# A two-layer transformer on one core: the rotation sums of the first attention issued behind the scores, and its output products cut into halves spread over the steps

## The chip, the cores and the metric

The kernel runs on one core of one Trainium2 chip. The metric is the device time of one execution in microseconds; three runs of the kernel before the change gave 754.88 to 755.31, median 755.07. All traces are of one profiled execution. The granted TensorE clock is full in every slice of it.

Engines are named as in the profile: PE is the matrix engine (PEld its weight loads), DVE the vector engine, ACT the scalar engine, POOL GpSimd, SP the engine that issues the DMAs.

## The reference, cut to what matters

Input x is 4 sequences of 256 tokens, 256 wide. Two layers follow one another, each an attention and a feed-forward block, each on the normed x and added to x. The change touches the first attention alone:

```python
q = einsum('btd,ndh->btnh', x, q_kernel)            # 16 query heads of 128
k, v = einsum('bsd,ckdh->cbskh', x, kv_kernel)      # 8 key/value heads of 128
q = apply_rope(rms_norm(q, q_norm_scale), positions)
k = apply_rope(rms_norm(k, k_norm_scale), positions)
# apply_rope: x1, x2 = halves of the head;  [x1*cos - x2*sin, x2*cos + x1*sin]
logits = einsum('btkgh,bskh->bkgts', qg * ATTN_SCALE, k)   # causal, window of 128
enc = einsum('bkgts,bskh->btkgh', softmax(logits), v)
out = einsum('btnh,nhd->btd', enc, out_kernel)             # 2048 -> 256, added to x
```

The remaining blocks (a gated feed-forward block with a 2-of-4 choice, a second causal attention, a gated block with a Walsh-Hadamard transform) come after it and are the same in both kernels.

## The kernel before, in words

Everything is f32. Each f32 matmul shows as two MATMUL entries in the trace, called passes here.

The first attention is `attention0`. Its work is cut into 16 units n = 4b + g: b is the sequence, g a group of four query heads with their two key/value heads. `pipelined` runs 20 steps. In step s, stage k works on unit s minus its lag, in a given order of stages, and then what `behind` holds for that step is issued. The order in which the code issues is a priority. The framework's scheduler makes of it one fixed order for each engine, and sets the semaphores; where `tc.issue_after(ins)` stands, an instruction is put behind `ins` on its engine.

The stages before the change, with lags:

- `project` (0), which calls `project0`: for both halves t of the tokens (128 each) two products `pj` (L426; four query heads, then keys and values). DVE multiplies them by the tables into `qs` and `qc` (L431), ACT squares them (L436) and copies `v` (L438). Then for both t: the rotation sum `qc += qs` with the halves of the head swapped (L443) and the sum of the squares `ss` (L444). For units from the seventh on (n >= 6) POOL splits the rotated queries into 16-bit planes `qpl` (L242, a helper's line) and SP transposes them by DMA to `qplT`. POOL then makes the norm factors `ve` (L457, L460) and `r` (L463, a power) and scales the keys, called K below (L466).
- `turn` (1), which calls `turn0`: queries by PE transposes `tr_q` (L481) and DVE copies (L482) for n < 6, by DVE copies out of `qplT` (L486) later; keys by PE transposes `tr_k` (L492) and ACT copies `kT` (L493).
- `score` (2): `probabilities` makes the scores `sc` (L204, L205). DVE adds the mask and takes the maximum in one pass, `mx` (L207). Then come `nb` (L214), exponentials on ACT (L217), the reciprocal `rs` (L222), and the scaling of `p` on POOL (L225).
- `split` (3): `p` into planes `pl` on POOL (L242), transposed by DMA to `plT`. `join` (4): copies to `pT` on ACT (L262); the last three units use PE transposes `tr_p` (L237) instead. `attend` (4): products `av` with the values (L380, L384), copied to `zT` by ACT (L388).

`out(b, t)` is the output product for one sequence and one half of its tokens: 16 matmuls (L294) over the four `zT` of the sequence, and one DVE addition to x (L299). `behind` puts these in steps 8, 9, 12 and 13 for the first two sequences; the four of the last two sequences stand at the end, in step 19, two of them as filler from the last projection on (`kept`).

PSUM has two pools of four banks each here: `half` (the `pj`, the `tr_q`, and `tr_k` for 6 <= n < 14) and `bank` (`sc`, `av`, `po`, `tr_n`, `tr_p`, and the other `tr_k`). The tiles `qc` have 4 buffers, `qs` and `sq` 2 each, `v` 5, `pl` and `plT` 4 together.

The order of the stages in a step is the last argument of `pipelined`: project, attend's `join`, `split`, `score`, `turn`, `attend`.

Of the kernel before, what the change touches and what calls it, by code (L numbers as in the profile page):

```python
# [27 lines left out]
P = 128  # L28
# [20 lines left out]
def two_layers(ctx, tc, consts, tables, x, wq, wkv, wo, w_gate, w_up, w_down,  # L49
# [26 lines left out]
    def bank(shape, name):  # L76
        return ps1.tile([P, *shape], F32, tag="bank", name=name)
# [238 lines left out]
    def attention0():  # L316
        with tc.tile_pool(name="attn0", bufs=2, reuse_waits="tile", side="right") as own:
            xnT, factors = {0: normed(0)}, {}


            cos_s = own.tile([P, NT, 2, HD], F32, name="cos_s", bufs=1)
            sin_s = own.tile([P, NT, 2, HD], F32, name="sin_s", bufs=1)
            with tc.issue_after(last_of["norm"].ins):
                for t in range(NT):
                    for tab, at in ((cos_s, 0), (sin_s, 256)):
                        src = angles[:, at + t * HD : at + (t + 1) * HD]
                        nc.vector.tensor_tensor(
                            tab[:, t], src.unsqueeze(1).to_broadcast([P, 2, HD]), scl, ALU.mult
                        )

            def project(n, _):
                b, g = divmod(n, 4)
                held = project0(own, xnT[b], g, cos_s, sin_s, n >= 6)
                if g == 1 and b + 1 < B:
                    factors[b + 1] = moments(b + 1)
                if g == 2 and b + 1 < B:
                    with tc.issue_after(last_of["qc"].ins):
                        xnT[b + 1] = normed(b + 1, factors[b + 1])
                return held

            def turn(n, held):
                rot, qT_planes, v, r = held
                return *turn0(own, rot, qT_planes, half if 6 <= n < 14 else bank), v, r

            def score(n, held):
                qT, kT, v, r = held
                ps = [
                    probabilities(
                        qT, kT, (2 * kk, 2 * kk + 1), mask0,
                        r[:, :, 2 * kk : 2 * kk + 2].rearrange("p t h -> p h t"),  # L350
                    )
                    for kk in range(2)
                ]
                return ps, v

            def split(n, held):
                ps, v = held
                return ps if n >= B * 4 - 3 else [
                    planes(p, own_planes) for p in ps
                ], v  # L360

            def own_planes(shape, name):
                return own.tile(shape, U16, tag="pl", name=name, bufs=4)

            def join(n, held):
                ps, v = held
                return [
                    transposed(ps[kk]) if n >= B * 4 - 3 else joined(ps[kk], ((
                        (nc.scalar.copy, slice(0, 2), last_of["exp"]),
                        (nc.scalar.copy, slice(0, 2), last_of["exp"]),  # L370
                    )[kk],)) for kk in range(2)
                ], v

            def attend(n, held):
                pTs, v = held
                zT = page("zT")
                for kk in range(2):
                    pT = pTs[kk]
                    av = bank([2, T], "av")
                    nc.tensor.matmul(  # L380
                        av, lhsT=v[:, 0, kk, :], rhs=pT[:, :, 0:T], start=True, stop=False,
                        skip_group_check=True,
                    )
                    nc.tensor.matmul(  # L384
                        av[:, :, P:T], lhsT=v[:, 1, kk, :], rhs=pT[:, :, T:],
                        start=False, stop=True, skip_group_check=True,
                    )
                    nc.scalar.copy(zT[:, 2 * kk : 2 * kk + 2, :], av)  # L388
                return zT

            def out(b, t, kept=False):
                def emit(done):
                    zTs = [done[4 * b + g] for g in range(4)]
                    if not kept:
                        project_out(bank([D], "po"), zTs, wo_sb, b, t)
                    else:
                        with tc.issue_after(last_of[0].ins):
                            project_out(half([D], "po"), zTs, wo_sb, b, t)
                return emit

            behind = {
                8: [out(0, 0)], 9: [out(0, 1)], 12: [out(1, 0)], 13: [out(1, 1)],
                17: [lambda _: xn_f.append(normed(0))],
                19: [lambda _: xn_f.append(normed(1)),
                     out(2, 0, True), out(2, 1, True), out(3, 0), out(3, 1)],
            }
            pipelined((project, turn, score, split, join, attend), (0, 1, 2, 3, 4, 4), behind, (0, 4, 3, 2, 1, 5))

    def project0(own, xnT, g, cos_s, sin_s, by_dma):


        v = own.tile([P, NT, 2, HD], F32, tag="v", name="v", bufs=5)
        r = small.tile([P, NT, 6], F32, tag="r", name="r")
        ss = small.tile([P, NT, 6], F32, tag="ss", name="ss")
        rot = []
        for t in range(NT):
            cols = slice(t * P, (t + 1) * P)
            sq = own.tile([P, 6, HD], F32, tag="sq", name="sq", bufs=2)
            qc = own.tile([P, 6, HD], F32, tag="qc", name="qc", bufs=4)
            qs = own.tile([P, 6, HD], F32, tag="qs", name="qs")  # L420

            for w, hs in ((wq_sb, slice(0, 4)), (wkv_sb, slice(4, 6))):
                pj = half([4, HD], "pj")
                n = hs.stop - hs.start
                for c in range(NC):
                    last_of[0] = nc.tensor.matmul(  # L426
                        pj, lhsT=xnT[:, c, cols], rhs=w[:, g, c, :],
                        start=(c == 0), stop=(c == NC - 1),
                    )
                for rot_to, tab in ((qs, sin_s), (qc, cos_s)):  # L430
                    last_of["qc"] = nc.vector.tensor_tensor(  # L431
                        rot_to[:, hs], pj[:, 0:n],
                        tab[:, t, hs.start // 4, :].unsqueeze(1).to_broadcast([P, n, HD]),
                        ALU.mult,
                    )
                nc.scalar.activation(sq[:, hs], pj[:, 0:n], AF.Square)  # L436
                if n == 2:
                    last_of["v", t] = nc.scalar.copy(v[:, t, :, :], pj[:, 2:4])  # L438
            rot.append((qc, qs, sq))
        for t, (qc, qs, sq) in enumerate(rot):  # L440

            parts = [i.rearrange("p n (s h) -> p n s h", s=2) for i in (qc, qs)]
            nc.vector.tensor_tensor(parts[0], parts[0], parts[1][:, :, ::-1, :], ALU.add)  # L443
            nc.vector.tensor_reduce(ss[:, t, :], sq, AX.X, ALU.add)  # L444
            rot[t] = qc
        qT_planes = None
        if by_dma:

            planes = page_of_planes([P, NT, 2, 4 * HD], "qpl")
            for t, qc in enumerate(rot):  # L450
                words = qc[:, 0:4, :].rearrange("p j h -> p (j h)").bitcast(U16)
                copy_gpsimd(planes[:, t], words.rearrange("p (n w) -> p w n", w=2))
            qT_planes = page_of_planes([P, NT * 2 * 4, P], "qplT")
            nc.sync.dma_start_transpose(qT_planes, planes.rearrange("p t w n -> p (t w n)"))

        ve = small.tile([P, NT, 6], F32, tag="ve", name="ve")
        nc.gpsimd.tensor_scalar(  # L457
            ve[:, :, 0:4], ss[:, :, 0:4], 1.0, HD * RMS_EPS, ALU.mult, ALU.add
        )
        nc.gpsimd.tensor_scalar(  # L460
            ve[:, :, 4:6], ss[:, :, 4:6], 1.0 / HD, RMS_EPS, ALU.mult, ALU.add
        )
        nc.gpsimd.tensor_tensor(r.rearrange("p t h -> p (t h)"), ve.rearrange("p t h -> p (t h)"),  # L463
                                mhalf, ALU.pow)
        for t, qc in enumerate(rot):
            last_of["k"] = nc.gpsimd.tensor_tensor(  # L466
                qc[:, 4:6, :], qc[:, 4:6, :],
                r[:, t, 4:6].unsqueeze(2).to_broadcast([P, 2, HD]), ALU.mult,
            )
        return rot, qT_planes, v, r  # L470

    def turn0(own, rot, qT_planes, bank_of_k):

# [474 lines left out]
```

## Time and profile before

| what | value |
|---|---|
| median of 3 runs | 755.07 us (754.88 to 755.31) |
| the profiled execution's own time | 755.64 us |
| its span | 753.8 us |
| PE busy | 738.6 us (98%) |
| PE weight loads busy | 601.4 us (80%) |
| DVE, ACT, POOL busy | 462.1, 399.7, 330.0 us (61%, 53%, 44%) |
| first product `pj` starts | 7.61 us |
| last sum of the first attention's long row of `po` starts | 268.02 us |

The profile page has the busy time of each engine, the span cut into 40 slices, and the groups of instructions with what ended the idle time ahead of them. A busy share of PE counts a pass until its modelled end, which overlaps the next one; the distance of the starts in the timeline tells more. The times between 7.6 and about 287 us belong to the first attention. What comes after it is the same in both kernels, in the same order on each engine.

### The profile page before, as it was taken

What the parts mean: (1) busy time and instruction counts of PE and PEld (TensorE: products, weight loads), DVE (VectorE), ACT (ScalarE), POOL (GpSimd) and SP (SyncE); (2) the same over time, 40 slices, a digit from 0 to 9 for tenths busy, and PEclk for the clock granted to TensorE, in tenths of its full rate; (3) what the DMA queues carried; (4) which work ended last, traced back from release to release, by engine and by line L of the source; (5) the groups of instructions that cost most, each with busy time, mean ns of one, the idle gap of its engine ahead of it and who ended that gap; (6) DMA issues with size and microseconds to landing.
All of it is one profiled execution on the core that took longest, in us unless ns stands there. A gap on an engine that the chain in (4) does not pass through costs nothing. (4 is left out here: it accounts for less than half of the span.)

```text
span 753.8 us, 11642 instructions
## 1 busy us (share of the span) xinstructions
PE 738.6 (98%) x3980; PEld 601.4 (80%) x3980; DVE 462.1 (61%) x1396; ACT 399.7 (53%) x985; POOL 330.0 (44%) x475
## 2 busy tenths in 40 slices
PE   8999999999999999999999999999999999999998
PEld 5556556656666788888899999999998899899997
DVE  6999886698678426987655644464443447344433
ACT  2378886678668722222346555555555675415332
POOL 1589998779678301011116433343338644220000
PEclk9999999999999999999999999999999999999999
DMA  8725445435433060001334422432232222002100
GB/s 322 284 42 71 69 86 100 82 59 108 73 70 71 1 223 14 16 15 22 119 70 84 127 43 43 98 100 43 43 71 43 43 43 42 2 0 22 27 10 28
DMA packets 121610, 53.30 MB, mean 71 GB/s; under 512 B 114768, under 2 KB 116944, under 8 KB 120784
## 3 DMA queue, kind: packets, MB, share of 16 engines
q1 hardware_dynamic: 121552, 52.57, 30.6%
q8 instruction: 31, 0.51, 0.3%
q14 instruction: 27, 0.22, 0.1%
HBM read 22.94 MB, written 1.05 MB: 32 GB/s over the span
## 5 line engine op out<-in xcount | busy, mean ns | idle before, releaser
L225 POOL TENSOR_SCALAR p<-p,rs 128x128 f32<-128x128 f32 (+1 forms) x256 | 120.9, 491 | 156.7 <-DVE rs L222 153.4
L207 DVE CUSTOM_DVE_ANT_0 p<-sc,cst 128x128 f32<-128x128 f32 (+1 forms) x256 | 78.7, 350 | 10.4 <-PE sc L205 7.8
L242 POOL TENSOR_SCALAR pl<-p 128x1536 uint16<-128x1536 uint16 x54 | 81.9, 1516 | 6.3 <-DMA plT<-pl 2.1
L262 ACT COPY pT<-plT 128x768 uint16<-128x768 uint16 (+1 forms) x54 | 77.1, 1486 | 1.8 <-DMA plT<-pl 1.8
L217 ACT ACTIVATE p<-p,nb,r 128x128 f32<-128x128 f32 (+1 forms) x128 | 68.2, 534 | 17.6 <-DVE nb L214 17.6
L426 PE MATMUL pj<-wq,xnT 128*128 128x512 f32 x128 | 61.8, 596 | 1.3 <-ACT xnT L179 0.7
L426 PE MATMUL pj<-wkv,xnT 128*128 128x512 f32 x128 | 60.9, 593 | 0.5 <-DMA wkv<-in_wkv_dram 0.5
L217 ACT ACTIVATE p<-p,nb 128x128 f32<-128x128 f32 (+1 forms) x128 | 56.3, 446 | 7.3 <-DVE nb L212 7.3
L282 PE MATMUL po<-w_o,zT 128*128 128x256 f32 x256 | 57.7, 379 | 0.0
L155 POOL TENSOR_SCALAR ve<-mv 128x2 f32<-128x2 f32 x16 | 3.4, 215 | 122.9 <-DVE mv L152 122.6
L294 PE MATMUL po<-wo,zT 128*128 128x256 f32 x256 | 57.2, 379 | 0.0
L294 PEld LDWEIGHTS po<-wo,zT 128*128 128x128 f32 x256 | 48.2, 190 | 6.3
L282 PEld LDWEIGHTS po<-w_o,zT 128*128 128x128 f32 x256 | 47.5, 190 | 5.8
L436 ACT ACTIVATE sq<-pj 128x512 f32<-128x512 f32 x64 | 29.6, 490 | 32.9 <-DVE qc L431 28.4
L426 PEld LDWEIGHTS pj<-wkv,xnT 128*128 128x128 f32 x128 | 23.8, 190 | 27.8 <-issue 24.4
L426 PEld LDWEIGHTS pj<-wq,xnT 128*128 128x128 f32 x128 | 23.0, 190 | 22.0 <-issue 17.8
L270 PE MATMUL av<-pT,v 128*128 128x256 f32 x128 | 38.9, 386 | 1.4 <-DVE mx L207 1.2
L222 DVE RECIPROCAL rs<-sm 128x4 f32<-128x4 f32 x64 | 11.2, 176 | 46.7 <-ACT p L217 46.1
L205 PE MATMUL sc<-kT,qT 128*128 128x256 f32 x128 | 38.2, 381 | 0.1
L205 PE MATMUL sc<-qk 128*128 128x256 f32 x128 | 38.2, 380 | 0.0
L632 ACT COPY qk<-qk_x 128x512 f32<-128x512 f32 x16 | 9.4, 586 | 53.8 <-PE qk_x L741 50.4
L463 POOL TENSOR_TENSOR r<-ve,mhalf 128x12 f32<-128x12 f32 x16 | 37.3, 2331 | 1.3
(154 smaller groups left out, 1773.3 us busy)
## 6 DMA issues: line engine op xcount, KB each, us to landing
w<-in_w_dram SPq DMA_DIRECT2D x3, 1024.0 KB, 4.8
wq<-in_wq_dram SPq DMA_DIRECT2D x4, 512.0 KB, 7.7
wkv<-in_wkv_dram SPq DMA_DIRECT2D x4, 512.0 KB, 8.0
wo<-in_wo_dram SPq DMA_DIRECT2D x4, 512.0 KB, 10.2
w_qk<-in_w_q_dram SPq DMA_DIRECT2D x4, 512.0 KB, 5.1
w_qk<-in_w_k_dram SPq DMA_DIRECT2D x4, 512.0 KB, 6.0
w_v<-in_w_v_dram SPq DMA_DIRECT2D x4, 512.0 KB, 7.2
w_o<-in_w_o_dram SPq DMA_DIRECT2D x4, 512.0 KB, 6.3
```

The costliest lines, as they stand in the source:

```text
L205: nc.tensor.matmul(sc[:, P : 3 * P], lhsT=q[:, P:T], rhs=k, start=True, stop=True)
L207: last_of["mx"] = nc.vector.tensor_tensor_reduce(out=p[:, j, cols], in0=sc[:, cols], in1=mask[:, cols], scale=1.0, scalar=-3.0e38, op0=ALU ...
L217: last_of["exp"] = nc.scalar.activation(p[:, j, cols], p[:, j, cols], AF.Exp, bias=nb[:, j, i : i + 1], scale=SCALE1 if rq is None else rq ...
L225: nc.gpsimd.tensor_scalar(p[:, j, cols], p[:, j, cols], rs[:, j, i : i + 1], 1.0, ALU.mult, ALU.mult)
L242: nc.gpsimd.tensor_scalar(o, i, 1.0, 1.0, ALU.mult, ALU.mult)
L262: copy(words.rearrange("p (n w) -> p w n", w=2), halves[:, :, js].rearrange("p w j n -> p w (j n)"),)
L270: nc.tensor.matmul(av, lhsT=v0, rhs=pT[:, 0:T], start=True, stop=False, skip_group_check=True)
L282: nc.tensor.matmul(po[:, t, :], lhsT=zT[:, j, t * P : (t + 1) * P], rhs=w[:, j, :], start=(t == j == 0), stop=(j == 3), skip_group_check=True,
L294: nc.tensor.matmul(po, lhsT=zTs[hd // 4][:, hd % 4, t * P : (t + 1) * P], rhs=w[:, hd, :], start=(hd == 0), stop=(hd == n - 1),)
L426: last_of[0] = nc.tensor.matmul(pj, lhsT=xnT[:, c, cols], rhs=w[:, g, c, :], start=(c == 0), stop=(c == NC - 1),)
L436: nc.scalar.activation(sq[:, hs], pj[:, 0:n], AF.Square)
L463: nc.gpsimd.tensor_tensor(r.rearrange("p t h -> p (t h)"), ve.rearrange("p t h -> p (t h)"), mhalf, ALU.pow)
```

## The change

Two things change, both in the order of the work; every product and sum of the first attention is still made.

First, the rotation sums, the sums of squares, the planes `qpl` with their DMA, the norm factors and K leave `project0` and become a stage `rotate` with `rotate0`, lag 0. The order in a step is now project, `join`, `split`, `score`, `rotate`, `turn`, `attend`: the sums stand behind the scores of the unit two before. For 2 <= n < 14 the two rotation sums are also placed behind the last `mx` on DVE.

Second, `out` takes a list of groups. An output product covers two groups (8 matmuls and one addition to x) and there is one in each step from 6 to 15: both halves of the tokens for groups 0 and 1 in steps 4b + 6 and 4b + 7, for groups 2 and 3 in steps 4b + 8 and 4b + 9. What would fall behind step 15 stays in step 19: groups 2 and 3 of the third sequence as filler, and the whole fourth sequence.

```diff
             def project(n, _):
                 b, g = divmod(n, 4)
-                held = project0(own, xnT[b], g, cos_s, sin_s, n >= 6)
+                held = project0(own, xnT[b], g, cos_s, sin_s)
...
+            def rotate(n, held):
+                rot, v = held
+                rot, qT_planes, r = rotate0(rot, n >= 6, last_of["mx"] if 2 <= n < 14 else None)
+                return rot, qT_planes, v, r
...
-            def out(b, t, kept=False):
+            def out(b, t, gs, kept=False):
+
                 def emit(done):
-                    zTs = [done[4 * b + g] for g in range(4)]
+                    zTs, w = [done[4 * b + g] for g in gs], wo_sb[:, 4 * gs[0] :]
                     if not kept:
-                        project_out(bank([D], "po"), zTs, wo_sb, b, t)
+                        project_out(bank([D], "po"), zTs, w, b, t)
                     else:
                         with tc.issue_after(last_of[0].ins):
-                            project_out(half([D], "po"), zTs, wo_sb, b, t)
+                            project_out(half([D], "po"), zTs, w, b, t)
                 return emit
 
             behind = {
-                8: [out(0, 0)], 9: [out(0, 1)], 12: [out(1, 0)], 13: [out(1, 1)],
-                17: [lambda _: xn_f.append(normed(0))],
-                19: [lambda _: xn_f.append(normed(1)),
-                     out(2, 0, True), out(2, 1, True), out(3, 0), out(3, 1)],
+                4 * b + 6 + 2 * k + t: [out(b, t, (2 * k, 2 * k + 1))]
+                for b in range(B) for k in range(2) for t in range(NT)
             }
-            pipelined((project, turn, score, split, join, attend), (0, 1, 2, 3, 4, 4), behind, (0, 4, 3, 2, 1, 5))
-
-    def project0(own, xnT, g, cos_s, sin_s, by_dma):
+            behind = {step: fns for step, fns in behind.items() if step < 16}
+            behind[17] = [lambda _: xn_f.append(normed(0))]
+            behind[19] = [
+                lambda _: xn_f.append(normed(1)), *(out(2, t, (2, 3), True) for t in range(NT)),
+                *(out(3, t, (0, 1, 2, 3)) for t in range(NT)),
+            ]
+            pipelined(
+                (project, rotate, turn, score, split, join, attend), (0, 0, 1, 2, 3, 4, 4),
+                behind, (0, 5, 4, 3, 1, 2, 6),
+            )
+
+    def project0(own, xnT, g, cos_s, sin_s):
...
             rot.append((qc, qs, sq))
+        return rot, v
+
+    def rotate0(rot, by_dma, first):
+
+        r = small.tile([P, NT, 6], F32, tag="r", name="r")
+        ss = small.tile([P, NT, 6], F32, tag="ss", name="ss")
         for t, (qc, qs, sq) in enumerate(rot):
 
             parts = [i.rearrange("p n (s h) -> p n s h", s=2) for i in (qc, qs)]
-            nc.vector.tensor_tensor(parts[0], parts[0], parts[1][:, :, ::-1, :], ALU.add)
+            with tc.issue_after(first.ins) if first else nullcontext():
+                nc.vector.tensor_tensor(parts[0], parts[0], parts[1][:, :, ::-1, :], ALU.add)
             nc.vector.tensor_reduce(ss[:, t, :], sq, AX.X, ALU.add)
             rot[t] = qc
...
-        return rot, qT_planes, v, r
+        return rot, qT_planes, r
```

In the fixed orders that come out of the scheduler, unit n's DVE work in a middle step of the new kernel reads: the products for t = 0, `ss` for t = 0, the products for t = 1, the eight `mx` of unit n - 2, the sum for t = 0, the sum for t = 1, `rs`, `ss` for t = 1, the two query copies of unit n - 1 with the second `rs`, and the addition to x. In the kernel before, both sums and both `ss` came ahead of the second of those eight `mx`, at most one `mx` ahead of them. On POOL a middle step reads: `qpl`, `qpl`, four `p`, `ve`, `pl`, four `p`, `r`, K, K, `pl`; before it read `qpl`, `qpl`, `ve`, `r`, K, K, four `p`, `pl`, four `p`, `pl` (the last `pl` at times between the next two `qpl`). On PE, `av` comes right behind `tr_k` and the output product right behind `av`; before, one `pj` matmul stood between `tr_k` and `av`.

## The prediction

> **What bounds the kernel now.** I read the page first, then who `av` waits for, then the timelines of PE and DVE around the longest of those waits, then the busy time by windows.
>
> ```profile
> PE 738.6 (98%) x3980; PEld 601.4 (80%) x3980; DVE 462.1 (61%) x1396; ACT 399.7 (53%) x985; POOL 330.0 (44%) x475
> ```
>
> PE fills the span; only time in which PE stands can be won. A busy share says little about that, so I take the starts of the PE timeline. In full rows a pass of 512 columns takes 0.43 us from start to start (four in 1.72), one of 256 takes 0.216 (32 in 6.91, at 118.67), one of 128 takes 0.109. What a start comes later than that is a gap. From 7.6 to 262 us the gaps over 0.03 us sum to 12.4 us.
>
> The `av` products (L380) wait most:
>
> ```profile
> its engine sat idle before it (us, times) until:
>   DVE mx L207: 12.1, 12
> ```
>
> (This adds PE's and PEld's idle time, so it is not PE's loss itself.) `av` needs one of four PSUM banks, and a bank comes free when DVE has read the scores in it. Step 11 on PE, and DVE at the same time:
>
> ```profile
> 166.74 0.60 PE L492 MATMUL tr_k<-cst,qc 128*128 128x128 f32 x4
> 167.18 1.02 PE L426 MATMUL pj<-wq,xnT 128*128 128x512 f32 x2
> 169.66 1.13 PE L380 MATMUL av<-pT,v 128*128 128x512 f32 x2 [1.46 <-DVE mx L207]
> ```
> ```profile
> 166.49 1.91 DVE L443 TENSOR_TENSOR qc<-qc,qs 128x768 f32<-128x768 f32 x1
> 168.33 0.94 DVE L444 TENSOR_REDUCE ss<-sq 128x6 f32<-128x768 f32 x1
> 169.19 0.41 DVE L207 CUSTOM_DVE_ANT_0 p<-sc,cst 128x256 f32<-128x256 f32 x1
> ```
>
> One sum and one `ss`, 2.7 us, stand ahead of the second `mx`; `av` starts 0.1 us after it. Which steps suffer shows in two windows, step 9 with its 16 output matmuls and step 11 without any (columns: busy us of PE, PEld, DVE, ACT, POOL, then clock):
>
> ```profile
> 126.70:146.00 19.30, 19.30 (x77) 13.40 (x76) 12.33 (x37) 13.62 (x29) 15.08 (x21) 1.00 0.45 83
> 166.00:180.00 14.00, 12.54 (x45) 7.08 (x44) 13.12 (x35) 11.31 (x29) 12.72 (x18) 1.00 0.49 91
> ```
>
> Without output matmuls PE has 12.5 us of work a step, and DVE and POOL as much; with 16 it has 19.4 and nothing else matters. **The rule against the row:** the Trainium skill, "Perfetto Trace Analysis", section "Identifying the Most-Contended Engine", says to judge PE's headroom by the busy share of weight loads. In step 11 that is 7.08 of 14.0, so half the step would be free, some 7 us. The starts give 1.62 + 0.10 here, and 1.17 + 0.10 at the same place in step 7. These are f32 passes, longer than the load they hide. I take the starts: the change can win 12.4 us at most, not a multiple.
>
> **The gaps, by place** (PE starts): start-up before 24 us, 2.0 with small ones (not touched). Steps 2 to 6: 0.48 (35.66), 1.27 (43.81), 0.31 (61.58), 0.69 (83.53), 0.41 (87.29): 3.2. At `av` and `pj` in the steps without output product and ahead of the first one behind them (steps 7, 8, 11, 12): 2.5 (102.25 to 116.5) and 2.5 (169.66 to 183.5): 5.0. The end from 235 us: 0.61, 0.36, 0.23, 0.10, 0.14, 0.13, 0.45: 2.0.
>
> **The output products.** The 128 matmuls (256 passes x 0.216 = 55 us) stay, so PE's work is unchanged. There are six more additions to x: 14 in place of 8, each 0.42 us (L299), 2.5 us of DVE. They lie under PE in steps that become PE-bound; uncovered, 2.5 us is their price. A step from 7 to 15 now has `pj` 6.88, `sc` 2.60, `tr_k` 0.44, `av` 2.58, output 3.46: **15.96 us of PE**, against 12.1 of DVE (products 3.7, two sums 1.9, two `ss` 1.7, `mx` and `nb` 2.5, `rs` 0.2, query copies 1.2, addition 0.4, slips 0.5), 12.3 of ACT and 12.7 of POOL. All get over 3 us of slack, where the steps without an output product had none.
>
> **The order on DVE.** I lay a middle step out from its first `pj`, with these durations. The scores end at 9.5, `mx` at 10.1, and the first `mx` of the step at 8.3, so `av`, due at 9.9, finds its bank. `po` wants its bank at 12.5, read by 9.0. The gaps of 5.0 us go. What is late next:
>
> - *The keys, with POOL's queue ahead of them.* K of unit n now stands behind eight `p` and a `pl`. First sum done at 11.0; then `qpl` 2 x 1.04, `p` 1.64, `ve` 0.54, `pl` 1.47, `p` 1.64, `r` 2.35, K 1.19: 10.9, so K at 21.9. `tr_k` is due at 9.5 of the next step, 25.4. Slack 3.5. Behind a late `tr_k` PE queues `av`, output and the next `pj`.
> - *SP and the planes.* `qpl` is done at 13.2; its transpose (median 4.7 us) lands near 18 and is read at 13 of the next step. `plT` of the unit behind it on SP's queue is issued near 17 and 23 and read at 15.5 of the next step. No wait.
> - *The squares.* `sq` has two buffers; `ss` for t = 1 frees one at 13, ACT refills it at 21. No wait. ACT now does `kT` behind the exponentials, at 14.4; the scores want it at 22.8.
>
> **The lock, rule and row.** This speaks against the change. The Trainium skill, "SBUF — State Buffer", section "Who interferes with whom": a DVE instruction with two SBUF inputs and a GpSimd one that reads SBUF exclude each other for the whole instruction, and so do DVE copies in a two-port mode. The trace has the first: beside two sums four `p` took 3.03 us, alone 1.64, and the longest `qpl` is 1.79 for 1.04.
>
> ```profile
> 44.87 3.03 POOL L225 TENSOR_SCALAR p<-p,rs 128x128 f32<-128x128 f32 x4
> ...
> 53.61 1.64 POOL L225 TENSOR_SCALAR p<-p,rs 128x128 f32<-128x128 f32 x4
> ```
> ```profile
> L242 POOL TENSOR_SCALAR qpl<-qc x20: 1040/1046/1787, 86.0 to 235.0; 128x1024 uint16<-128x1024 uint16 x20
> ```
>
> In the new order the second sum meets `qpl`, and the query copies meet the first four `p`. By the row that is 0.7 us (1.79 less 1.04), K's slack 2.8; by the rule, blocking in full, 0.9 and 1.2, slack 1.4. No row has query copies beside `p`: bounds 0 and 1.2. I take the rule's 1.2, but both leave K in time, so the sum is the same: no gap. DVE can lose a us itself; it has three.
>
> **Steps 2 to 6 give something back.** Here queries go by `tr_q`, which hold two of four `half` banks until DVE copies them out (L482), and these copies now stand behind sums and `ss` (4.4 us) instead of right behind `mx`. Following starts from 31.75: the scores of unit 0 and 1 come earlier and the 3.2 us go, but the second half of `pj(3)` waits 0.85 for a copy, that of `pj(4)` 1.55, and the transposes of unit 5 wait 0.95 for ACT's squares, which are behind plane copies. Together 3.35: a net of -0.1. Bounds: if no copy were late, +3.2; if each of the five steps lost 1 us more to locked sums (recorded 1.91 for 0.94), -5. I take zero.
>
> **The end.** The second sum of unit 15 stands behind all `mx` now, about 1 us later from the last `pj`, but `mx` of unit 13, on which ACT's chain (exponentials 4.3, key copy, `zT`, two `pT` of 1.85) starts, comes 2 us earlier. Eight output matmuls fewer are left (56 against 64), of which fewer are filler. I take the 2.0 us of gaps as gone but 0.6 for scores of unit 15 waiting for banks: +1.4, bounds 0 and 2.
>
> **The sum.** 5.0 + 0 + 1.4 = 6.4 us won. Against the profiled execution: 753.8 - 6.4 = 747.4 of span, with 1.84 around it 749.2; that execution lay 0.57 above the median, so **748.7 us**. The attention's end moves from about 287 to about 281, and everything later moves with it: its inputs are long there, its order is the same.
>
> **The rivals.**
>
> *Keys late (slower).* If POOL's ops in the new order all take their long recorded times (`qpl` 1.79 twice, `p` 3.03 twice, `pl` 2.06, K 1.90), K is 5.6 later, at 27.5, and `tr_k` stands 2.1 us. It decides from a chain of 14.4 us between first sum and K. The loop runs over two steps: chain 16.5, then `tr_k`, `av`, output, `pj` 13.4, then DVE to the next first sum 4: 33.9, 16.95 a step for 15.96, and over nine steps 9 us lost. 748.7 + 9 = 758. For it: the rule, and POOL at 12.7 of 14 in step 11. Against: in 16 us a lock seldom hits every op. 0.13.
>
> *The early steps eat it (about equal).* DVE is busy 19.4 of 20 us from 40 to 60. If each of steps 2 to 6 loses the 1 us above, 753.8. For it: the copies behind the sums. Against: DVE was as full before and PE stood 3.2 us. 0.13.
>
> *Only half happens.* In units 14 and 15 the first sum still stands ahead of `mx`; elsewhere the fixed order has both behind, so this rival is only that gaps return at another bank or buffer: 751.5. 0.22.
>
> *Forecast,* gaps of steps 6 to 15 gone: 747 to 750.5. 0.52.
>
> **How the numbers follow.** The likeliest time is 748.7. The range takes the forecast, the third case and most of the second, and the start of the first: 746.8 to 755.0, leaving out the late keys and a tenth of the rest. A measurement of this kernel tells about 0.2%, 1.5 us, from no change. Faster by more (under 753.6): all of forecast and third, a third of the second: 0.78. Slower by more (over 756.6): late keys nearly whole, 0.12. Between: 0.10.
>
> **What would show it.** Right: `av` no longer waits for DVE `mx`; output rows of 3.46 us in each step from 6 to 15; `sc` to `sc` near 16.0 us there; long row of `po` at the end near 263 for 268; `pj` gaps around 39, 50 and 82. Wrong: `tr_k` waiting for POOL K, `p` near 3 us in each step, or the scores of unit 5 later than 101 (then the early steps failed).

## The result, and the profile after

The changed kernel takes **749.96 us** (median of 6 runs, 749.57 to 750.22) against 755.12 before (6 runs, 754.88 to 755.31). The ratio is 0.9932, with a 95% interval of 0.9919 to 0.9945: 5.2 us, about 0.7%, faster. The prediction said 748.7, with a range from 746.8 to 755.0. The profiled execution has a span of 748.1 us for 753.8.

The first row of the page shows that PE holds a little more of a shorter span, and that DVE has six more instructions, the six additions to x:

```profile
PE 737.5 (99%) x3980; PEld 603.2 (81%) x3980; DVE 465.9 (62%) x1402; ACT 401.6 (54%) x985; POOL 331.0 (44%) x475
```

What the first `av` product (now L385) waits for has shrunk from 12 entries to 2, one place in step 5 (the second entry is the weight load of the same wait):

```profile
its engine sat idle before it (us, times) until:
  DVE mx L207: 1.9, 2
```

Step 11 in the PE timeline, the step in which PE stood 1.72 us at `av` before, runs without a gap:

```profile
165.92 0.38 PE L204 MATMUL sc<-kT,qT 128*128 128x128 f32 x2
...
168.54 0.60 PE L510 MATMUL tr_k<-cst,qc 128*128 128x128 f32 x4
168.98 1.02 PE L385 MATMUL av<-pT,v 128*128 128x512 f32 x2
...
171.56 3.62 PE L294 MATMUL po<-wo,zT 128*128 128x256 f32 x16
175.01 1.88 PE L437 MATMUL pj<-wq,xnT 128*128 128x512 f32 x4
...
181.88 0.38 PE L204 MATMUL sc<-kT,qT 128*128 128x128 f32 x2
```

From scores to scores it is 15.96 us, the forecast's figure. The same stretch by engines (busy us of PE, PEld, DVE, ACT, POOL, then the clock) leaves DVE 3.5 us and POOL 3.9 us idle, where the window of step 11 before left them 0.9 and 1.3:

```profile
165.92:181.88 15.96, 15.96 (x61) 10.40 (x60) 12.43 (x36) 11.93 (x28) 12.10 (x16) 1.00 0.58 108
```

I sum the gaps on PE by starts again, as the prediction did, over three stretches: early (from 24 us to 2.6 us after the first scores of unit 5), middle (from there to the first scores of unit 13) and end (from there to the first matmul of the feed-forward layer).

| us | early | middle | end | span |
|---|---|---|---|---|
| before | 3.6 | 5.2 | 2.3 | 753.8 |
| after | 3.6 | 1.3 | 0.9 | 748.1 |

The gain is 3.9 in the middle and 1.4 at the end, 5.3 of the 5.7 us by which the span is shorter; from the first matmul of the feed-forward layer on, the two kernels stay 5.6 to 5.7 us apart. The three gaps over half a microsecond that are left (PE timeline; the time in brackets is the wait that the profile puts down to a releaser):

```profile
50.80 1.55 PE L437 MATMUL pj<-wq,xnT 128*128 128x512 f32 x3 [0.92 <-DVE qT L500]
...
72.77 1.13 PE L385 MATMUL av<-pT,v 128*128 128x512 f32 x2 [0.83 <-DVE mx L207]
...
148.76 1.01 PE L510 MATMUL tr_k<-cst,qc 128*128 128x128 f32 x4 [0.43 <-POOL qc L484]
```

### The profile page after: what moved, and what is told of

Same layout as the page of the kernel before. It is cut to its first block, busy times and chain, and to the rows that moved or that the text cites. A ratio compares the mean times of both kernels' runs of the same rounds, so it can differ in the third digit from the quotient of the medians.

```text
span 748.1 us, 11666 instructions
## 1 busy us (share of the span) xinstructions
PE 737.5 (99%) x3980; PEld 603.2 (81%) x3980; DVE 465.9 (62%) x1402; ACT 401.6 (54%) x985; POOL 331.0 (44%) x475
## 4 chain that ended last, share of the span: by engine, by line
PE 42%; POOL 3%; DVE 2%; ACT 2%; DMA 1%; issue 1%; POOLq 0%
PE po L282 6%; PE qk_x L759 6%; PE gu_x L829 4%; PE po_f L587 4%; PE av L270 3%; PE qk_y L759 3%; PE sc L205 3%; PE v_x L765 3%; PE v_zy L765 2%; PE gu_y L829 2%; PE av L273 2%; PE sc L204 1%; POOL w_qkt L805 1%; PE qk_z L759 1%; ACT p L217 1%; PE gu_z L829 1%
## 5 line engine op out<-in xcount | busy, mean ns | idle before, releaser
L225 POOL TENSOR_SCALAR p<-p,rs 128x128 f32<-128x128 f32 (+1 forms) x256 | 116.8, 474 | 157.7 <-DVE rs L222 154.2
L242 POOL TENSOR_SCALAR pl<-p 128x1536 uint16<-128x1536 uint16 x54 | 79.5, 1473 | 3.5
L442 DVE TENSOR_TENSOR qs<-pj,sin_s 128x512 f32<-128x512 f32 x64 | 35.3, 552 | 13.9 <-PE pj L437 13.5
L644 DVE TENSOR_TENSOR qk<-qk_y,u 128x512 f32<-128x512 f32 x16 | 11.1, 692 | 43.6 <-PE qk_y L759 42.5
```

Of the source, the lines that this page charges most:

```text
L225: nc.gpsimd.tensor_scalar(p[:, j, cols], p[:, j, cols], rs[:, j, i : i + 1], 1.0, ALU.mult, ALU.mult)
L242: nc.gpsimd.tensor_scalar(o, i, 1.0, 1.0, ALU.mult, ALU.mult)
```

## The experiments

Times of a run are compared through the runs of the kernel before on the same chip (medians 754.72 to 754.95). The gaps of all kernels, in the stretches of the table above, are put together here. The time is the median of a kernel's runs, the gaps are those of its profiled execution; where PE ran at a lower clock, the longer passes count as gaps.

| kernel | time | ratio to before (95%) | early | middle | end |
|---|---|---|---|---|---|
| before | 755.12 | 1 | 3.6 | 5.2 | 2.3 |
| changed | 749.96 | 0.9932 (0.9919 to 0.9945) | 3.6 | 1.3 | 0.9 |
| order only | 764.44 | 1.0125 (1.0106 to 1.0143) | 3.5 | 14.5 | 3.9 |
| spread only | 753.56 | 0.9982 (0.9974 to 0.9989) | 4.0 | 3.8 | 1.5 |
| no rule of issue | 752.67 | 0.9971 (0.9960 to 0.9983) | 5.3 | 2.2 | 0.9 |
| copies first | 751.90 | 0.9962 (0.9949 to 0.9974) | 5.4 | 1.3 | 1.0 |
| `r` twice | 765.71 | 1.0141 (1.0127 to 1.0155) | 3.5 | 12.6 | 6.4 |
| `tr_k` of unit 9 later | 751.06 | 0.9956 (0.9943 to 0.9968) | 3.5 | 2.4 | 1.0 |
| copies on ACT | 751.39 | 0.9951 (0.9938 to 0.9963) | 4.9 | 1.3 | 1.0 |
| queries by DMA from unit 5 | 751.37 | 0.9958 (0.9944 to 0.9972) | 7.5 | 1.3 | 0.9 |
| old place early | 749.50 | 0.9932 (0.9919 to 0.9944) | 3.4 | 1.3 | 0.9 |
| `ve` three times | 758.82 | 1.0057 (1.0045 to 1.0070) | 3.5 | 6.7 | 6.1 |
| K ahead of `p` | 750.59 | 0.9946 (0.9933 to 0.9958) | 3.3 | 1.6 | 1.7 |
| K ahead of `p`, copies first | 751.59 | 0.9957 (0.9944 to 0.9971) | 4.2 | 1.3 | 1.7 |

### The two parts of the change, each alone

**Order only.** The rotation stage of the changed kernel, the output products as they were.

```
-            behind = {4 * b + 6 + 2 * k + t: [out(b, t, (2 * k, 2 * k + 1))] ...}
+            behind = {8: [out(0, 0)], 9: [out(0, 1)], 12: [out(1, 0)], 13: [out(1, 1)], ...}
```

> The sums stand behind mx as in the changed kernel, the output products stay at 16 matmuls in steps 8, 9, 12 and 13 and none in 6, 7, 10 and 11. By the prediction's own layout (K at 21.9 us after the first pj of its step, tr_k due at 9.5 + 12.5 = 22.0 in a step without output matmuls) the order alone takes the gaps away: about 749 to 750 us. By the changed kernel's trace K comes at 23.9, so a pair of steps without output work cannot be shorter than 23.9 + 3.0 (tr_k, av) = 26.9 us for 25.0 of PE work, twice: tr_k waits for POOL K there, near 2 us in each pair, and the time is about 752 to 753. If the order does nothing and the even spread everything: 755.

It is 9.5 us slower than before. K waits appear in the short steps, twice as large as expected, and something new behind them (PE timeline; then the windows, with the granted clock as the third number from the end):

```profile
114.91 0.59 PE L505 MATMUL tr_k<-cst,qc 128*128 128x128 f32 x2 [2.53 <-POOL qc L479]
116.19 0.69 PE L505 MATMUL tr_k<-cst,qc 128*128 128x128 f32 x2 [0.69 <-POOL qc L479]
116.67 1.92 PE L385 MATMUL av<-pT,v 128*128 128x512 f32 x2
```
```profile
116.20:121.90 5.70, 5.70 (x11) 3.28 (x12) 4.20 (x6) 5.70 (x18) 5.70 (x5) 0.50 0.37 69
...
188.00:193.70 5.70, 5.70 (x11) 3.29 (x12) 3.37 (x4) 3.86 (x8) 5.70 (x7) 0.51 0.41 76
```

PE stands 2.69 and 1.00 us by starts for K of unit 7, and then runs 5.7 us at half its clock: two passes of 512 columns take 1.71 us from start to start in place of 0.86. That costs another 2.8 us. The same happens at 186.64. So the new order is no gain by itself: without output matmuls a step is too short for K's new place.

**Spread only.** The kernel before with the new output products.

```
-                8: [out(0, 0)], 9: [out(0, 1)], 12: [out(1, 0)], 13: [out(1, 1)],
+                4 * b + 6 + 2 * k + t: [out(b, t, (2 * k, 2 * k + 1))]
+                for b in range(B) for k in range(2) for t in range(NT)
```

> The kernel before with the output products spread, eight matmuls in each step from the seventh on; the sums stay ahead of the second mx. If the spread alone gives DVE the slack that it needs, the steps from 7 to 12 have no gaps: about 750 us, the early gaps of 3.2 us as before. If av still meets a bank that DVE has not read, because one sum and one ss are ahead of mx however long the step is, a part of each gap of 1.2 to 1.7 us stays, some 0.5 us in each of nine steps: 752 to 754, with av waiting for DVE mx in most steps.

It wins 1.4 us. `av` still waits, with 13 entries in place of 12, and the DVE and PE timelines of one step say why:

```profile
  DVE mx L207: 8.6, 13
```
```profile
185.32 0.95 DVE L448 TENSOR_TENSOR qc<-qc,qs 128x768 f32<-128x768 f32 x1
186.19 0.94 DVE L449 TENSOR_REDUCE ss<-sq 128x6 f32<-128x768 f32 x1
187.05 0.41 DVE L207 CUSTOM_DVE_ANT_0 p<-sc,cst 128x256 f32<-128x256 f32 x1
```
```profile
187.53 1.13 PE L380 MATMUL av<-pT,v 128*128 128x512 f32 x2 [0.25 <-DVE mx L207]
```

DVE had nothing to do for over 3 us of this step, and still it is late: the sum and `ss` (1.7 us) stand ahead of the second `mx` at the same point of each step. Slack in sum did not repair the order. A step is 16.48 us here and 15.96 in the changed kernel; the 0.52 is this wait (0.42 and 0.10). The two parts alone make +9.5 and -1.4 us, together -5.2. Each removes what the other one suffers from.

**No rule of issue.** The changed kernel with `first` set to None.

```
-                rot, qT_planes, r = rotate0(rot, n >= 6, last_of["mx"] if 2 <= n < 14 else None)
+                rot, qT_planes, r = rotate0(rot, n >= 6, None)
```

> The changed kernel without the rule that the first sum of units 2 to 13 is issued behind the last mx; the stage stands at the same place. If that rule makes the order, sums come ahead of mx again and av waits for DVE mx in most steps: 751.5 to 753 us, like the spread alone. If the place of the stage is enough: 750.

752.7, as if the rule made the order, but not by the expected wait. The rule does decide where the first sum stands: without it the first sum of every unit from 5 on runs ahead of all eight `mx` (the changed kernel has it behind them up to unit 13). The second sum stays behind them, but for units 6 and 10. In the middle `av` waits for `mx` in one step only (1.73 us at 187.65), and there the first sum is long, beside K and `pl` on POOL (DVE timeline of two steps, then POOL):

```profile
115.96 0.97 DVE L461 TENSOR_TENSOR qc<-qc,qs 128x768 f32<-128x768 f32 x1
119.62 0.28 DVE L207 CUSTOM_DVE_ANT_0 p<-sc,cst 128x128 f32<-128x128 f32 x1
...
180.42 3.91 DVE L461 TENSOR_TENSOR qc<-qc,qs 128x768 f32<-128x768 f32 x1
```
```profile
180.89 1.20 POOL L484 TENSOR_TENSOR qc<-qc,r 128x256 f32<-128x256 f32 x2
182.04 1.49 POOL L242 TENSOR_SCALAR pl<-p 128x1536 uint16<-128x1536 uint16 x1
```

Most of the loss, 1.7 us, is in the early steps, where the sum at 45.99 takes 3.25 us in the same company. So, by this run and the one before, what the order has to avoid is a sum and `ss` just ahead of the second `mx`; a first sum that ran before the scores made `av` wait in that one step alone. That the long sums make the loss is read from the rows; no run here tests it.

### How much room K has

**`r` twice.** K comes 2.28 us later for units 6 to 15.

```
-        nc.gpsimd.tensor_tensor(r..., ve..., mhalf, ALU.pow)
+        for _ in range(2 if by_dma else 1):
+            nc.gpsimd.tensor_tensor(r..., ve..., mhalf, ALU.pow)
```

> The changed kernel with r (POOL, 2.28 us) computed twice for units 6 to 15, so K comes 2.28 us later. By the prediction's layout K has 3.5 us to spare: no change, 750.0. By the changed kernel's trace it has 1.7 to 2.1: K at 23.9 + 2.28 = 26.2 after the first pj of its step, and the loop K, tr_k, av, output, pj of two steps takes 26.2 + 6.5 = 32.7 us for 31.9: 0.4 us lost in each of some eight steps, 753.2, with tr_k waiting for POOL K in steps 8 to 15.

The kernel loses 15.8 us against the changed one, not 3. Who `tr_k` waits for, and the clock behind the longest of these waits (3.30 us at 152.83):

```profile
  POOL qc L485: 26.3, 24
```
```profile
152.80:158.70 5.90, 5.87 (x18) 4.18 (x19) 2.38 (x7) 1.88 (x5) 5.50 (x7) 0.50 0.36 67
```

**`ve` three times.** K comes 1.07 us later, within the slack of 1.7 to 2.2 us that K has for units 7, 8, 11, 12 and 14 (unit 13 has 0.9 to 1.3, unit 9, in step 10, none, units 6 and 10 over 6).

```
+        for _ in range(3 if by_dma else 1):
             nc.gpsimd.tensor_scalar(ve[:, :, 0:4], ss[:, :, 0:4], 1.0, HD * RMS_EPS, ALU.mult, ALU.add)
             nc.gpsimd.tensor_scalar(ve[:, :, 4:6], ss[:, :, 4:6], 1.0 / HD, RMS_EPS, ALU.mult, ALU.add)
```

> The changed kernel with the two short ve operations (0.27 us each from start to start) three times for units 6 to 15, so K comes 1.07 us later. K has 1.7 to 2.1 us to spare in steps 8 to 15, only in step 10 none: if that slack is real and the 16 us that the double r cost come only from going past it, this costs the wait of step 10 alone, 1 us: 751. If any delay of K is passed on: some 7 us by the share of 1.07 to 2.28, 757.

758.8, 9 us more than the changed kernel: the slack is not a slack. For unit 7 K is 1.22 us later than in the changed kernel (this execution runs 0.34 us ahead there, which is allowed for) and the first `tr_k` still has 0.86 us to spare; for unit 8 it is 2.35 later and `tr_k` waits. Where the second 1.1 us comes from shows on POOL and DVE in the step between:

```profile
118.21 1.47 POOL L242 TENSOR_SCALAR pl<-p 128x1536 uint16<-128x1536 uint16 x1
```
```profile
118.41 1.28 DVE L214 SCALAR_TENSOR_TENSOR nb<-mx,r 128x4 f32<-128x4 f32 x1
```

`nb` multiplies 128 x 4 numbers and takes 0.16 us in most steps. Here it starts 0.20 us into POOL's `pl`, takes 1.28 us, and ends at 119.69, 0.01 us after `pl`. Behind it on DVE stand the last three `mx` and both sums, so the next K is as much later again. In the changed kernel the same pair just passes: at 118.74 `nb` takes 0.16, and that step's `pl` runs from 117.33 to 118.80. In the step after, K and the `pl` behind it are later still, and now `pl` meets the first sum itself (0.95 us in the changed kernel):

```profile
135.30 1.47 POOL L242 TENSOR_SCALAR pl<-p 128x1536 uint16<-128x1536 uint16 x1
```
```profile
135.60 1.97 DVE L461 TENSOR_TENSOR qc<-qc,qs 128x768 f32<-128x768 f32 x1
```

Unit 9's K is then 2.5 us later, so the delay comes back about doubled, through `nb` in one step and through the sum in another. Of the ten `nb` over 0.3 us in this run, each ends when an instruction of POOL ends. Behind a wait of 2.39 us in step 10 and one of 2.73 at the end the clock is halved as well.

**K ahead of `p`.** Only POOL's order is another: K ahead of the first `pl` and the second four `p`.

```
+                while waiting:                      # the second four p
+                    with tc.issue_after(last_of["k"].ins):
+                        waiting.pop(0)()
...
+                with tc.issue_after(last_of["k"].ins) if n < 13 else nullcontext():
                     return [planes(p, own_planes) for p in ps], v
```

> The changed kernel with another order on POOL alone: K ahead of the first pl and the second four p (3.1 us) in steps 2 to 15. If POOL's queue sets K, it comes 3.1 us earlier: tr_k has 5 us to spare in steps 8 to 15, and the 0.9 us of step 10 go, though tr_n, which then asks for xn earlier, may take part of it back: 749.1 to 750. Otherwise 750. If the p and pl that are now later make pT late: av waits for ACT pT, 751 or more.

K has 4.8 to 5.3 us to spare in the middle steps in place of 1.7 to 2.2, and nothing is won: 750.6. Its slack was not what bounds the changed kernel; POOL's queue does set it. Step 10 still loses, to others:

```profile
148.19 1.13 PE L448 MATMUL pj<-wq,xnT 128*128 128x512 f32 x2 [0.32 <-ACT sq L458]
149.97 0.76 PE L177 MATMUL tr_n<-cst,xn 128*128 128x128 f32 x4 [0.66 <-DVE xn L170]
```

### The gap of step 10

**`tr_k` of unit 9 later.** In step 10, where the third sequence is normalized, `tr_k` stands ahead of the scores and meets K; here it goes behind them.

```
+            with tc.issue_after(last_of["sc"].ins) if n == 9 else nullcontext():
                 for j in range(2):
                     nc.tensor.transpose(tk[:, j, :], qc[:, 4 + j, :], ident)
```

> The changed kernel with the tr_k of unit 9 issued behind the scores of unit 8, as it is for the other units. Its waits for POOL K in step 10 (0.59 and 0.30 us at 149) go: 749.1, or 748.8 if the 0.29 of tr_n goes with them. If something else is late there instead (the scores themselves, or DVE's xn), 750.

751.1, and a span of 748.9 for 748.1, so nothing is won: the waits at `tr_k` (0.89 us) are gone, and larger ones stand at the transposes of `xn`:

```profile
149.22 0.44 PE L177 MATMUL tr_n<-cst,xn 128*128 128x128 f32 x2 [1.17 <-DVE xn L170]
...
150.70 0.44 PE L177 MATMUL tr_n<-cst,xn 128*128 128x128 f32 x2 [0.81 <-DVE xn L170]
```

`tr_k` had been filling a wait for DVE. With the run before this settles the place: in step 10 of the changed kernel `sq` (149.05), K (149.28) and `xn` (150.92) come within 1.9 us of each other, and taking away one shows the next. The `xn` pair takes 1.88 us there, beside a `pl` from 149.25 to 150.78; the pair that follows takes 0.73.

### The early steps

**Old place early.** The sums of units 0 to 5 as before, the new place from unit 6 on.

```
                 held = project0(own, xnT[b], g, cos_s, sin_s)
+                if n < 6:
+                    held = (*rotate0(held[0], False, None), held[1])
```

> The changed kernel with the sums of units 0 to 5 left where they were before (ahead of mx), only units 6 to 15 in the new place. The prediction took steps 2 to 6 at nothing: 3.2 us of gaps gone, 3.3 given back. Then this kernel stands within 0.7 us of the changed one, 750.0 to 750.7, with the old gaps at 35.7, 43.8 and 83.5 in place of those at 50.8 and 72.8. If the new place is worse there than the old: 748 to 749.

749.5, the same ratio as the changed kernel. The old gaps are back (1.15 us for the scores of unit 1 at 43.01, for example) and those at 50.80 and 72.77 gone: 3.4 against 3.6 us. So the early steps gave back what they won, as the prediction had put it, and the whole gain is from unit 6 on.

**Copies first, copies on ACT, K first and copies first, queries by DMA.** Four attempts on those 3.6 us. The query stage ahead of the sums in steps 0 to 5:

```
-                behind, (0, 5, 4, 3, 1, 2, 6),
+                behind, (0, 5, 4, 3, 1, 2, 6) if step >= 6 else (0, 5, 4, 3, 2, 1, 6),
```

> The changed kernel with the query stage ahead of the rotation stage in steps 0 to 5, where queries go by tr_q. If the gaps of pj(3) and pj(4) (0.46 and 1.18 us) come from query copies that stand behind sums and ss, they go, and av(1)'s 1.1 us in step 5 with them if DVE is early there: 747.5 to 748.5 us. If what DVE does later in those steps is only moved (sums later, so K later and tr_k waiting), as much comes back: 750, with tr_k waiting for POOL K in steps 3 to 5.

The gaps at `pj` and `av` go, and K is late (PE timeline):

```profile
60.49 0.44 PE L510 MATMUL tr_k<-cst,qc 128*128 128x128 f32 x2 [1.11 <-POOL qc L484]
61.78 0.44 PE L510 MATMUL tr_k<-cst,qc 128*128 128x128 f32 x2 [0.85 <-POOL qc L484]
```

The same with K ahead of `pl` and the second `p` on POOL (the edits of both kernels together):

> The last kernel, and in steps 0 to 5 the query copies ahead of the sums on DVE. The copies alone took away the gaps of pj and av there (2.7 us) and paid with tr_k waits of 4.3 us; with K ahead on POOL those should shrink: 746.5 to 748. If the first sums, not POOL's queue, made K late in these steps, the tr_k waits of 4 us stay: 751.5.

`tr_k` waits 0.6 us in these steps in place of 4.4, so POOL's queue was the cause. But then the squares and `xn` of step 6 are late:

```profile
81.79 1.18 PE L510 MATMUL tr_q<-cst,qc 128*128 128x128 f32 x8 [0.93 <-ACT sq L458]
...
85.65 0.44 PE L177 MATMUL tr_n<-cst,xn 128*128 128x128 f32 x2 [0.81 <-DVE xn L170]
```

The second query copy of units 2 to 5 on ACT:

```
-                nc.vector.tensor_copy(qT[:, :, cols], tq)
+                (nc.scalar.copy if n >= 2 and t else nc.vector.tensor_copy)(qT[:, :, cols], tq)
```

> The changed kernel with the second query copy of units 2 to 5 (0.68 us of DVE, from tr_q) on ACT. If DVE's lateness makes the early gaps (pj(4) 1.18, av(1) 1.1), about half goes: 748.8. If the half bank now waits for ACT, whose queue has exponentials and key copies ahead of that copy, pj waits for ACT instead: 750 to 751.5.

`av` of unit 1 waits 0.2 in place of 1.0, but the 1.0 of `pj(4)` stays, and 1.9 us come at `tr_q` and `tr_n` of step 6. Last, one more unit by DMA:

```
-                rot, qT_planes, r = rotate0(rot, n >= 6, ...)
+                rot, qT_planes, r = rotate0(rot, n >= 5, ...)
...
-                return *turn0(own, rot, qT_planes, half if 6 <= n < 14 else bank), v, r
+                return *turn0(own, rot, qT_planes, half if 5 <= n < 14 else bank), v, r
```

> The changed kernel with the queries of unit 5 by DMA (it is from unit 6 on before). PE loses eight tr_q, 0.87 us of work, and the 0.4 us of gaps around 83 to 85 that stand at them; POOL gets two qpl (2.1 to 3.2 us) in step 5. With room on POOL (K of unit 5 has 3.7 to 5.7 us to spare): 748.7. If POOL's delay makes K or the p of unit 3 late: 750 or more, with tr_k or av waiting for POOL or a plane transpose.

`tr_k` of unit 5 waits 3.13 us for K, and the clock falls behind it:

```profile
85.00:88.40 3.40, 3.40 (x8) 1.84 (x9) 0.95 (x1) 1.29 (x4) 3.09 (x6) 0.58 0.00 0
```

From 36 to 78 us DVE is busy 13.5 to 13.9 of each 14 us in both the kernel before and the changed one, and each edit moves the wait to whichever of copies, squares, K and `xn` is last. None of the twelve kernels is measurably faster than the changed one.

## Why the prediction was right, point by point

- **What bounds it.** PE by its starts, not by the busy share of its weight loads: right. PE had 12.4 us of gaps to give, and 5.7 came. In step 11 of the changed kernel, which has no gap at all, weight loads are busy 10.40 of 15.96 us (65%). (The section of the Trainium skill that the prediction cites, "Identifying the Most-Contended Engine" in "Perfetto Trace Analysis", names MFU, the matmul work against the peak, beside that share; the prediction left MFU out, and it was not worked out here.)
- **The middle, 5.0 us forecast.** 3.9 came. `av` finds its bank in all steps from 6 to 15, and steps of 15.96 us are exactly the sum of PE's rows. The step of the prediction that failed is its layout of "a middle step", taken for all of them: step 10 has the `tr_n` of the next sequence, and there `tr_k` is issued ahead of the scores, 2.6 us earlier. It costs 0.59 and 0.30 at `tr_k`, 0.29 at `tr_n` and some small ones, 1.3 in all. The 1.1 us that the middle fell short are most of the 1.26 us between forecast and result.
- **Both parts are needed.** The prediction gave one sum for them. Alone they are +9.5 and -1.4 us. Its reason for the order (sum and `ss` ahead of the second `mx`) is shown by the spread alone, its reason for the spread (slack) by the order alone, for K on POOL; that DVE needed slack too is not shown.
- **K, 3.5 us of slack forecast, 2.8 by the row and 1.4 by the rule.** 1.7 to 2.2 measured in most steps, 0.9 to 1.3 for unit 13. K ends 23.9 us after the first `pj`, forecast 21.9. The locks make most of the 2.0: `qpl` beside the second sum and the copies takes 3.23 in place of 2.08, the first four `p` beside the copies 2.06 in place of 1.64, as one step of the changed kernel's POOL shows.

```profile
170.40 3.23 POOL L242 TENSOR_SCALAR qpl<-qc 128x1024 uint16<-128x1024 uint16 x2 [3.55 <-issue]
173.61 2.06 POOL L225 TENSOR_SCALAR p<-p,rs 128x128 f32<-128x128 f32 x4
...
177.76 1.64 POOL L225 TENSOR_SCALAR p<-p,rs 128x128 f32<-128x128 f32 x4
179.36 2.28 POOL L481 TENSOR_TENSOR r<-ve,mhalf 128x12 f32<-128x12 f32 x1
181.72 1.19 POOL L484 TENSOR_TENSOR qc<-qc,r 128x256 f32<-128x256 f32 x2
```

  That is 1.6 us of lock, between row (0.7) and rule (2.1), and like both it leaves K in time in the middle steps but step 10.
- **The rival "keys late"** was given 0.13 and did not come, but its terms were mis-sized. It was to decide from a chain of 14.4 us between first sum and K, and to cost 9 us when K is 5.6 late. The chain measured 12.65 us in the changed kernel for units 7 to 9, 11 and 12. At 13.9 (`ve` three times) it already costs 9 us, at 15.0 (`r` twice) it costs 16. Two things were missing: `nb` and the first sum, which are held up by `pl` when K is late, so that a delay comes back about doubled; and the half clock behind the long waits. That `nb` and the sum are the links is read from their rows; a kernel without that meeting was not tried.
- **Steps 2 to 6, forecast at nothing.** Right: 3.6 and 3.6 us of gaps, and the same time with the old place there. The forecast's own pieces were 0.85, 1.55 and 0.95 at `pj(3)`, `pj(4)` and `tr_q(5)`; measured 0.46, 1.18 and 0.2 (0.3 more at the `tr_n` behind it). In place of the rest came a wait that it did not have, `av` of unit 1 in step 5. Again it is `nb` behind a `pl`:

```profile
70.89 1.47 POOL L242 TENSOR_SCALAR pl<-p 128x1536 uint16<-128x1536 uint16 x1
```
```profile
71.32 1.06 DVE L214 SCALAR_TENSOR_TENSOR nb<-mx,r 128x4 f32<-128x4 f32 x1
```

  `nb` ends at 72.37, `pl` at 72.36; the `mx` behind `nb` frees the bank at 72.7, and `av` starts at 72.77. So this part of the sum was right by pieces that were wrong in both directions, which is luck.
- **The end, 1.4 us forecast.** 2.3 to 0.9, 1.4 measured, but this too is luck in part: the 0.6 us left were forecast at the scores of unit 15, and 0.45 of the 0.9 stand at `tr_p`, as before the change (259.24 before, 256.20 after). The spread alone gives 0.8 of the 1.4; what gives the rest was not tested.
- **The markers.** Output rows of 3.46 us in each step, 15.96 from scores to scores, the gaps at 39, 51 and 83 and the unit-5 scores at 100.3 (forecast: not later than 101) all came. `av` no longer waits for `mx`, but for the one place in step 5. The long row of `po` came at 264.99, 2 us later than forecast (near 263). `tr_k` waiting for POOL's K was named as a sign of failure; it came, in one step.

## What to carry to other kernels

An order and a fill can be worth nothing or worse apart and pay together: the order took away a fixed lateness of DVE, the fill gave POOL the time that the order had taken, so test both alone before crediting either. The slack that one trace shows on a chain over several engines need not be there when the chain is delayed: before counting on 2 us, look for instructions on it, short ones too, that a long one of another engine would then meet, and try a small delay, as `ve` three times did. When a gap is taken away and another of its size opens next to it, as in the early steps and in step 10, several chains end there together; none of the six orders and moves tried in those two places won anything, and less work there was not tried.

## What the runs showed of the hardware

- **Short DVE instructions pay for long ones of GpSimd.** `nb` has two SBUF inputs and 128 x 4 elements, 0.16 us in the median. The Trainium skill, "SBUF — State Buffer", section "Who interferes with whom", says that such an instruction and a GpSimd one that reads SBUF exclude each other for the whole instruction. The runs agree: in all kept traces each `nb` over 0.3 us ends within 0.03 us of an instruction of POOL, and the longest took 1.50 us. What I had not expected is that the smallest instruction on the chain can be one of those that decide.
- **PE's clock fell behind long gaps.** In the profiled executions of four kernels the granted clock was 0.50 to 0.71 over the 3 us behind seven gaps of 2.39 to 3.30 us by starts, a pass of 512 columns 0.85 us apart in place of 0.43. Behind the six gaps of 1.43 to 1.93 us in the kept traces it stayed at 1.00. So a wait of 3.3 us cost 3.3 and 2.9 more (5.9 us at 0.50). A limit is not shown by this. Two of the five executions of `tr_k` of unit 9 later have a mean clock of 0.998 and take 752.7 and 753.0 us, the others 750.7 to 751.1, though the longest gap behind the start-up in its trace is 1.33 us, with one of 0.98 close behind. And one of the five of queries by DMA has the full clock and takes 750.5, the others 751.2 to 753.5 at 0.995 to 0.998. Only one execution of each kernel has a trace, so where the clock fell in the others is open.
